# Eight of sixteen activation differences behind the last LSTM step: VectorE subtraction, or ScalarE negation and an adding DMA

## The chip, the cores and the metric

The kernel runs on one core of a Trainium2 chip. The time is the device time of one execution in microseconds (us). The kernel before was run three times: 306.83, 307.32 and 307.53 us, with a median of 307.32.

The core has five engines, each with an instruction queue of its own that runs in order: TensorE (PE: matrix products into the PSUM banks), VectorE (DVE), ScalarE (ACT), GpSimd (POOL) and SyncE (SP). Transfers (DMAs) are issued from the queues of SP, ACT and POOL and run by 16 DMA engines that all queues share. Semaphores hold an instruction back until what it needs is done; everything behind it in the same queue waits too.

## The reference

An LSTM over 64 time steps for 32 sequences with 256 hidden units, then a feed-forward net of three layers with weights of +1 and -1, and a residual:

```python
def step(carry, xw_t):
    prev_h, prev_c = carry
    a = xw_t + prev_h @ Wh
    i = sigmoid(a[:, :H]); f = sigmoid(a[:, H:2*H])
    o = sigmoid(a[:, 2*H:3*H]); g = tanh(a[:, 3*H:])
    next_c = f * prev_c + i * g
    next_h = o * tanh(next_c)
...
h = concatenate([y, -y], axis=-1)          # y: (32, 64, 256), the LSTM's output
h = relu(s0 * (h @ sign(k0))) * 2          # 512 -> 1024
h = relu(s1 * (h @ sign(k1))) * 2          # 1024 -> 1024
return x + s2 * (h @ sign(k2))             # 1024 -> 256
```

## The kernel before

**Blocks.** The 64 steps fall into four blocks of 16 steps; a block is 16 x 32 = 512 columns for the feed-forward net. The 64 recurrent steps run one after the other, and the products of the feed-forward net for blocks that are done are dealt out between them, as one long generator from which each step takes its share. The order of all instructions is written out by hand by that generator; each engine executes its own in that order.

**The last two blocks** are computed together by `last_blocks`. There, layer 1 (1024 to 1024) of both blocks is a product of a 2 x 2 matrix of weight quarters with a 2 x 2 matrix of activations, and is done with seven quarter products in place of eight (the Strassen-Winograd form). The activations are the layer-0 results: `f[k, 0]` for the third block and `f[k, 1]` for the fourth, k from 0 to 7, each a tile of 128 x 512 float32 (256 KB). With b11, b21 the lower and upper four tiles of the third block and b12, b22 those of the fourth, the form needs four differences, each of four tiles (K2 = 4), so sixteen in all:

- t1 = b12 - b11, written over `f[k, 0]`, k < 4 (L542)
- t2 = b22 - t1, in tiles of its own, `t2[k]` (L545)
- t3 = b22 - b12, written over `f[i, 1]`, i < 4 (L576)
- t4 = b21 - t2, written over `f[4 + i, 0]` (L586)

All four are made by `differ`, a VectorE subtraction (its records carry the line of the helper, L464).

**Splits.** Each operand of a product goes into TensorE as two float32r tiles, a high part and a low part. `split` (L481) makes them: a ScalarE cast into the high part (records at L482), and a VectorE subtraction, operand minus high, for the low part (again L464). The low part is issued one split later (`later`, L471), so that VectorE need not wait for the cast just before it.

**Order of the products behind the last step.** With four q banks, two banks that had held the gates, and two more (named r): t2's products into q0 to q3 (L573), then t1's into the same banks (L583), t3's into the four r banks (L594), t4's into the same (L601), b22's into q again (L607). Each product is eight matmuls (four parts, high and low) of 128 x 512. Between them:

- `u[i]` (L575) is a ScalarE copy of `q[i]` behind t2's product; t1's product then accumulates on in the same bank, so it must wait for the copy. `v[i]` (L585) is a copy of the same bank behind t1's product.
- `take_sum` (L496) adds `r[i]` to `v[i]` on VectorE (L497) behind t3's product; t4's product then accumulates on in r, and waits for that sum. The result goes through ReLU on ScalarE (L492) and a low part on VectorE (L493).
- layer 2 follows: the `po` products at L617 and L629, the output sums (L637) and the stores.

ScalarE's queue in this stretch, in order: the copies of `p1` into q2 and q3 (L560), four casts of t1, then for each i the copy `u[i]` and the cast of t3's part i, then for each i the copy `v[i]` and the cast of t4's part i, then casts of b22 mixed with the ReLUs of the sums.

GpSimd issues seven small loads at the start and computes some scales until about 12 us; its queue is empty from there to the end. SP issues the loads of the residuals (L96 by `load_x`, L565) just ahead of this stretch.

Of the kernel before, what the change touches and what calls it, by code (L numbers as in the profile page):

```python
# [37 lines left out]
AF = mybir.ActivationFunctionType  # L38
ALU = mybir.AluOpType
# [4 lines left out]
def lstm_ffn(ctx: ExitStack, tc: tile.TileContext, x, cond, wx_d, wh_d, b_d, k0_d, k1_d, k2_d, s0_d, s1_d, s2_d, out):  # L44
    nc = tc.nc
# [38 lines left out]
    def act(shape, dtype, name):  # L84
        return apool.tile(shape, dtype, tag="act", name=name)
# [312 lines left out]
    K2, F2 = FC0 // 2, F1 // 2  # L398
# [21 lines left out]

    f, parts = {}, {"b11": {}, "b21": {}}

    def layer0(p, m, hi, lo):
        for n, (k, a) in enumerate(((0, hi), (0, lo), (1, hi), (1, lo))):
            nc.tensor.matmul(p, w0[:, k, ts(m, P)], a[:, k, :], start=(n == 0), stop=(n == 3))  # L425
            if n < 3:
                yield 1

    def first_chunk(b, m):

        p = ps_f.tile([P, TB], F32, tag="pf", name=f"p0_{b}_{m}")
        yield from layer0(p, m, *hparts[b])
        f[m, 0] = act([P, TB], F32, f"f0_{m}")
        h, l = (act([P, TB], F32R, f"b{m}{s}") for s in "hl")
        load[0] += 1
        nc.scalar.activation(f[m, 0], p, AF.Relu)
        nc.scalar.copy(h, f[m, 0])
        nc.vector.tensor_tensor(l, f[m, 0], h, ALU.subtract)
        parts["b11" if m < K2 else "b21"][m % K2] = h, l
        yield 1  # L440

    def last_blocks(b):
# [6 lines left out]
        def product(bank, i, a, b, first=False):  # L449
            for k in range(K2):  # L450
                for n in range(2):
                    nc.tensor.matmul(  # L452
                        bank,
                        a(k)[:, ts(i, P)],
                        b[k][n],
                        start=first and k == 0 and n == 0,
                        stop=k == K2 - 1 and n == 1,
                        skip_group_check=True,
                    )
                    if not (k == K2 - 1 and n == 1):  # L460
                        yield 1

        def differ(out, in0, in1):
            nc.vector.tensor_tensor(out, in0, in1, ALU.subtract)  # L464

        def pair(name):
            return [act([P, TB], F32R, f"{name}{s}") for s in "hl"]
# [3 lines left out]
        def later(low):  # L471

            late.append(low)
            if len(late) > 1:
                late.popleft()()
# [5 lines left out]
        def split(a, h, l):  # L481
            nc.scalar.copy(h, a)  # L482
            later(lambda: differ(l, a, h))

        def large(name):

            both = [wpool.tile([P, K2, TB], F32R, tag=tag, name=f"{name}{tag}") for tag in ("wh", "w0")]
            parts[name] = [[t[:, k] for t in both] for k in range(K2)]
# [41 lines left out]
        t2 = [hpool.tile([P, 2, TB], F32, tag=tag, name=f"t2{tag}") for tag in ("hhi", "hlo")]  # L530
        t2 = [t2[k // 2][:, k % 2] for k in range(K2)]
        parts["t2"] = {}
        for n, m in enumerate(m for k in range(K2) for m in (k, K2 + k)):
            if n % 4 == 0:
                banks = four_banks(f"p0_{b + 1}_{n}_")
            p = banks[n % 4]
            yield from layer0(p, m, hi, lo)
            f[m, 1] = act([P, TB], F32, f"f1_{m}")
            nc.scalar.activation(f[m, 1], p, AF.Relu)
            k = m % K2  # L540
            if m < K2:
                differ(f[k, 0], f[k, 1], f[k, 0])  # L542
                yield 1
                continue
            differ(t2[k], f[m, 1], f[k, 0])  # L545
            for j in {0: [], K2 - 1: [k - 1, k]}.get(k, [k - 1]):
                parts["t2"][j] = pair(f"t2_{j}")
                split(t2[j], *parts["t2"][j])
            yield 1
            if k == 0:  # L550
                yield from second(1)
            else:
                settle()
            if k == 2:
                nc.scalar.copy(q[1], p1[1])
# [8 lines left out]
        for i in range(NQ):  # L564
            nc.sync.dma_start(out=res[i // 2][:, i % 2], in_=x_in[:, ts((b + 1) * NQ + i, SH)])  # L565

        large("t1")
        for k in range(K2):
            split(f[k, 0], *parts["t1"][k])
# [2 lines left out]
        for i in range(K2):  # L572
            yield from product(q[i], i, lambda k: sums[2, k], parts["t2"])  # L573
            u[i] = act([P, TB], F32, f"u{i}")
            nc.scalar.copy(u[i], q[i])  # L575
            differ(f[i, 1], f[K2 + i, 1], f[i, 1])  # L576
            parts["t3"][i] = pair(f"t3_{i}")
            split(f[i, 1], *parts["t3"][i])
            yield 1

        parts["t4"] = {}
        for i in range(K2):
            yield from product(q[i], i, lambda k: sums[1, k], parts["t1"])  # L583
            v[i] = act([P, TB], F32, f"v{i}")
            nc.scalar.copy(v[i], q[i])  # L585
            differ(f[K2 + i, 0], f[K2 + i, 0], t2[i])  # L586
            parts["t4"][i] = pair(f"t4_{i}")
            split(f[K2 + i, 0], *parts["t4"][i])
            yield 1
# [54 lines left out]
    def layer0_chunk(b, m):  # L644
        if b == NB - 2:
            yield from first_chunk(b, m)
            return
        p = ps_f.tile([P, TB], F32, tag="pf", name=f"p0_{b}_{m}")
        yield from layer0(p, m, *hparts[b])
        a0s[b, m] = evict(p, f"a0_{b}_{m}")  # L650
        yield 1
# [98 lines left out]
    def ffn():  # L750
        for b in range(NB - 2):
            yield from ffn_block(b)
        yield from last_blocks(NB - 2)
# [80 lines left out]
```

## Time and profile before

| | |
|---|---|
| median of three runs | 307.32 us |
| the profiled execution's own time | 307.09 us |
| its span on the core | 305.3 us |
| last recurrent step's matmuls (L308) end | about 232.5 us |
| t2's products into q | 249.27 to 256.52 us |
| t1's products into q | 256.52 to 263.77 us |
| t3's products into r | 263.77 to 271.03 us |
| t4's products into r | 271.03 to 278.28 us |
| b22's products into q | from 278.28 us |
| last matmul ends | 300.6 us |

The times are from the start of the span. The stages are read from the timeline of TensorE, as the start of the first matmul of each. The profile shows busy time for each engine; a matmul's record lasts 0.39 us, but the next starts 0.227 us after it, since they overlap. The chain that ended last is followed back from the last instruction: at each step to what released it, or to the instruction before it on its engine.

### The profile page before, as it was taken

What the parts mean: (1) busy time and instruction counts of PE and PEld (TensorE: products, weight loads), DVE (VectorE), ACT (ScalarE), POOL (GpSimd) and SP (SyncE); (2) the same over time, 40 slices, a digit from 0 to 9 for tenths busy, and PEclk for the clock granted to TensorE, in tenths of its full rate; (3) what the DMA queues carried; (4) which work ended last, traced back from release to release, by engine and by line L of the source; (5) the groups of instructions that cost most, each with busy time, mean ns of one, the idle gap of its engine ahead of it and who ended that gap; (6) DMA issues with size and microseconds to landing.
All of it is one profiled execution on the core that took longest, in us unless ns stands there. A gap on an engine that the chain in (4) does not pass through costs nothing.

```text
span 305.3 us, 9553 instructions
## 1 busy us (share of the span) xinstructions
PE 299.3 (98%) x4010; PEld 233.8 (77%) x4010; DVE 187.8 (62%) x527; ACT 154.9 (51%) x526; POOL 6.6 (2%) x24
## 2 busy tenths in 40 slices
PE   8999999999999999999999999999999999999993
PEld 4988887787777777777777777777777888888893
DVE  2476767676774565666575746444456689796341
ACT  0224657784565654444453544655676688644100
POOL 5300000000000000000000000000000000000000
PEclk9999999999999999999999999999999999999999
DMA  6865001133000000000001000000001330000012
GB/s 182 210 181 114 20 10 48 32 84 84 4 0 2 2 2 1 2 2 1 2 2 38 19 18 2 0 2 3 3 0 37 91 83 0 0 0 2 0 51 88
DMA packets 27450, 10.87 MB, mean 36 GB/s; under 512 B 23560, under 2 KB 26632, under 8 KB 27408
## 3 DMA queue, kind: packets, MB, share of 16 engines
q1 hardware_dynamic: 24768, 8.66, 11.5%
q10 hardware_dynamic: 2400, 1.57, 1.8%
q8 instruction: 31, 0.51, 0.7%
q0 software_dynamic: 240, 0.04, 0.1%
q14 instruction: 11, 0.09, 0.1%
HBM read 8.16 MB, written 2.10 MB: 34 GB/s over the span
## 4 chain that ended last, share of the span: by engine, by line
PE 98%; DVE 0%; issue 0%
PE p L679 21%; PE gates L308 20%; PE px L249 18%; PE q L452 12%; PE p L425 9%; PE po L666 5%; PE po L629 2%; PE gates L452 2%; PE po L617 2%; PE r L452 2%; PE gates L425 1%; PE p_idle L708 1%; PE gates L706 0%; DVE o L637 0%; PE p_bias L723 0%; DVE idle L113 0%
## 5 line engine op out<-in xcount | busy, mean ns | idle before, releaser
L308 PEld LDWEIGHTS gates<-wh,hist 128*32 128x32 f32 x2016 | 54.6, 109 | 22.3 <-issue 7.8
L308 PE MATMUL gates<-wh,hist 128*32 128x192 f32 x2016 | 68.1, 275 | 0.0
L249 PE MATMUL px<-wx,xT 128*32 128x256 f32 (+1 forms) x1168 | 60.5, 353 | 0.1
L249 PEld LDWEIGHTS px<-wx,xT 128*32 128x32 f32 x1168 | 42.4, 110 | 11.4 <-DVE c_first L717 0.8
L325 ACT ACTIVATE sig<-gates 128x128 f32<-128x128 f32 x64 | 17.7, 277 | 60.7 <-PE gates L308 60.4
L329 DVE TENSOR_TENSOR kept<-sig,c 128x64 f32<-128x64 f32 x63 | 14.2, 225 | 32.4 <-ACT sig L325 32.1
L335 ACT ACTIVATE th<-c 128x64 f32<-128x64 f32 x64 | 16.4, 257 | 32.2 <-DVE c L333 32.2
L337 DVE TENSOR_TENSOR h<-sig,th 128x64 f32<-128x64 f32 x64 | 14.4, 225 | 20.7 <-ACT th L335 20.7
L265 DVE TENSOR_TENSOR xg<-px,bias 128x512 f32<-128x512 f32 x32 | 21.2, 671 | 2.8 <-PE px L249 2.3
L425 PE MATMUL p<-hlo,w 128*128 128x512 f32 x56 | 22.5, 402 | 0.0
L425 PE MATMUL p<-hhi,w 128*128 128x512 f32 x56 | 22.3, 399 | 0.0
L319 ACT COPY gates<-xg 128x192 f32<-128x192 f32 x64 | 20.0, 313 | 0.6 <-DVE xg L265 0.6
L342 DVE STREAM_TRANSPOSE hist<-h 128x64 f32<-128x64 f32 x64 | 15.7, 246 | 2.6
L333 DVE TENSOR_TENSOR c<-kept,new 128x64 f32<-128x64 f32 x64 | 14.4, 225 | 2.2
L327 ACT ACTIVATE sig<-gates 128x64 f32<-128x64 f32 x64 | 14.9, 233 | 0.1
L331 DVE TENSOR_TENSOR new<-sig,cand 128x64 f32<-128x64 f32 x64 | 14.0, 218 | 0.0
L326 ACT ACTIVATE cand<-gates 128x64 f32<-128x64 f32 x64 | 14.0, 218 | 0.0
L320 ACT COPY gates<-xg 128x64 f32<-128x64 f32 x64 | 13.0, 203 | 0.0
L425 PEld LDWEIGHTS p<-hlo,w 128*128 128x128 f32 x56 | 10.5, 188 | 2.5
L425 PEld LDWEIGHTS p<-hhi,w 128*128 128x128 f32 x56 | 10.5, 188 | 2.4
L214 ACT ACTIVATE w<-bits,nsgn,sgn 128x1024 fp32r<-128x1024 uint8 x8 | 9.9, 1241 | 0.0
L362 DVE TENSOR_TENSOR hlo<-hist,hhi 128x256 fp32r<-128x256 f32 x16 | 7.5, 468 | 2.6 <-ACT hhi L361 2.6
(361 smaller groups left out, 573.4 us busy)
## 6 DMA issues: line engine op xcount, KB each, us to landing
x<-in_x_dram SPq DMA_DIRECT2D x52, 64.0 KB, 2.7
out_dram<-o SPq DMA_DIRECT2D x28, 64.0 KB, 1.8
bits<-in_L_ffn_k_dram SPq DMA_DIRECT2D x10, 128.0 KB, 3.4
wx<-in_L_cond_Wx_dram SPq DMA_DIRECT2D x2, 256.0 KB, 4.4
wx<-in_L_cond_Wx_dram ACTq DMA_DIRECT2D x4, 128.0 KB, 5.3
wh<-in_L_cond_Wh_dram ACTq DMA_DIRECT2D x2, 256.0 KB, 6.1
wh<-in_L_cond_Wh_dram SPq DMA_DIRECT2D x2, 256.0 KB, 6.8
k<-in_L_ffn_k_dram SPq DMA_DIRECT2D x2, 256.0 KB, 3.0
```

Of the source, the lines that this page charges most:

```text
L249: nc.tensor.matmul(p[q * N : (q + 1) * N, t % 2, slots], xT[i // 2, i % 2][:, s, k, :], wx_q[:, k, q, slots], start=start, stop=False, ski ...
L265: nc.vector.tensor_tensor(xg[t], p.rearrange("p t g j -> p t (g j)"), b, ALU.add)
L308: nc.tensor.matmul(g[q * N : (q + 1) * N], hT[:, k, :], wh_q[:, k, q, slots], start=False, stop=(k == 1), skip_group_check=True,)
L319: nc.scalar.copy(gates[0], x_t[:, :3])
L325: nc.scalar.activation(sig[:, 0:2, :], gates[0][:, 1:3], AF.Sigmoid)
L327: nc.scalar.activation(sig[:, 2, :], gates[1][:, 0], AF.Sigmoid)
L335: nc.scalar.activation(th, c, AF.Tanh)
L342: nc.vector.transpose(hT, h.rearrange("p (j b) -> p b j", b=2))
L425: nc.tensor.matmul(p, w0[:, k, ts(m, P)], a[:, k, :], start=(n == 0), stop=(n == 3))
L452: nc.tensor.matmul(bank, a(k)[:, ts(i, P)], b[k][n], start=first and k == 0 and n == 0, stop=k == K2 - 1 and n == 1, skip_group_check=True,)
L666: nc.tensor.matmul(po[m], w2[:, m, k], a1[k][n], start=(k == 0 and n == 0), stop=(k == FC1 - 1 and n == 1))
L679: nc.tensor.matmul(p1[m], w1[:, k, ts(m, P)], a0[k][n], start=(k == 0 and n == 0), stop=(k == FC0 - 1 and n == 1),)
```

## The change

The eight VectorE subtractions that make t3 and t4 are taken out. In place of each stands a ScalarE instruction that multiplies one operand by -1 in place, and a DMA, issued from GpSimd's queue, that reads one SBUF tile and adds it to another SBUF tile.

- t3: `f[i, 1]` is negated and `f[4 + i, 1]` is added to it. All four negations and DMAs are written ahead of the casts of t1.
- t4: `t2[i]` is negated and added to `f[4 + i, 0]`. These are written in the loop over t2's products, each behind the cast of t3's part i.

The four differences of t1 and the four of t2 stay on VectorE. The products and their order stay.

```diff
+    def negate(a):
+        nc.scalar.activation(a, a, AF.Copy, scale=-1.0)
+
+    def add_to(a, b):
+        nc.gpsimd.dma_start(out=a, in_=b, accum_op=ALU.add)
...
+        for i in range(K2):
+            negate(f[i, 1])
+            add_to(f[i, 1], f[K2 + i, 1])
         large("t1")
         for k in range(K2):
             split(f[k, 0], *parts["t1"][k])
...
             yield from product(q[i], i, lambda k: sums[2, k], parts["t2"])
             u[i] = act([P, TB], F32, f"u{i}")
             nc.scalar.copy(u[i], q[i])
-            differ(f[i, 1], f[K2 + i, 1], f[i, 1])
             parts["t3"][i] = pair(f"t3_{i}")
             split(f[i, 1], *parts["t3"][i])
+            negate(t2[i])
+            add_to(f[K2 + i, 0], t2[i])
             yield 1
...
             yield from product(q[i], i, lambda k: sums[1, k], parts["t1"])
             v[i] = act([P, TB], F32, f"v{i}")
             nc.scalar.copy(v[i], q[i])
-            differ(f[K2 + i, 0], f[K2 + i, 0], t2[i])
             parts["t4"][i] = pair(f"t4_{i}")
             split(f[K2 + i, 0], *parts["t4"][i])
             yield 1
```

In the program's order, ScalarE's queue becomes: the L560 copies, four negations, four casts of t1, then for each i: copy `u[i]`, cast of t3's part i, negation of `t2[i]`; then, as before, `v[i]` and the cast of t4's part i. Each cast of t3 and t4, and each low part of them on VectorE, waits for the DMA of its tile. GpSimd's queue gains eight DMAs behind its work at the start, each waiting for its negation.

## The prediction

> **What bounds the kernel now.** I read the page's busy shares and its chain that ended last, then, for the stretch behind the last step, the chain in order of time, then windows of five microseconds, then the timelines of ScalarE (ACT), VectorE (DVE) and GpSimd (POOL).
>
> ```profile
> PE 299.3 (98%) x4010; PEld 233.8 (77%) x4010; DVE 187.8 (62%) x527; ACT 154.9 (51%) x526; POOL 6.6 (2%) x24
> PE 98%; DVE 0%; issue 0%
> 245.80 18.13 PE q L452 x80
> 263.94 3.63 PE gates L452 x16
> ```
>
> TensorE (PE) is the bound: the chain is 98% its matmuls, and the last two lines, of the chain in order of time, show where the change sits: 80 matmuls in 18.13 us, 0.2267 us each, with no gap. They are the layer-1 products into q; the products into the banks called gates and r follow.
>
> ```profile
> 255.00:260.00 5.00, 5.00 (x24) 4.14 (x23) 5.00 (x10) 4.56 (x9) 0.00 (x0) 1.00 0.00 0
> 260.00:265.00 5.00, 5.00 (x24) 4.14 (x23) 3.62 (x6) 3.26 (x8) 0.00 (x0) 1.00 0.00 0
> 285.00:290.00 5.00, 5.00 (x24) 4.14 (x23) 1.39 (x3) 0.60 (x1) 0.00 (x0) 1.00 0.00 0
> ```
>
> Columns: stretch, length, then busy time of PE, weight load, DVE, ACT, POOL, granted clock, DMA share. DVE is full from 255 to 260, ACT nearly, and yet PE runs as many records (24) as from 285 to 290, where DVE does 1.39 us. So relieving DVE can't make PE faster: PE neither waits for it here nor slows beside it. DMA is empty throughout: new transfers meet no others.
>
> ```profile
> 250.15 1.26 ACT L560 COPY q<-p 128x512 f32<-128x512 f32 x2
> 251.35 2.18 ACT L482 CAST t1wh<-f 128x512 fp32r<-128x512 f32 x4
> 253.43 0.58 ACT L575 COPY u<-q 128x512 f32<-128x512 f32 x1
> 254.53 0.62 ACT L482 CAST t_0h<-f 128x512 fp32r<-128x512 f32 x1 [0.52 <-DVE f L464]
> 255.05 0.58 ACT L575 COPY u<-q 128x512 f32<-128x512 f32 x1
> ```
>
> This is the ACT queue into which the change goes. The cast of t3's part 0 follows the u0 copy, and u1 follows it. The u copies matter: each empties a q bank into which PE's t1 products accumulate again.
>
> **When PE wants its inputs** (start of the first matmul, PE timeline): q0 for t1 at 256.52, q1 at 258.33, q2 at 260.15, q3 at 261.96; t3's parts from 263.77 to 265.36; the bank of r0 for t4 at 271.03, then every 1.81 us.
>
> **The change, part by part.**
>
> Removed: eight DVE subtractions (L464, 0.69 us long, 0.605 from start to start), 4.8 us of DVE. By the windows above this buys nothing.
>
> Added, ACT: four negations ahead of the t1 casts and one behind each t3 cast. The nearest rows are the 128x512 casts and copies, 0.53 us from start to start; bounds 0.52 and 0.65 (spacing of the L482 and L560 pairs). The first four push t1's casts from 251.35 to 253.47 and u0 from 253.43 to about 255.6, ending 256.2; PE wants q0 at 256.52. Cost nothing with 0.3 us of cover, at most 0.2 by the 0.65. The t1 casts end near 255.7 and their DVE lows near 256.5, each ahead of its matmul (the last low is due at 258.11). The later four make ACT's loop (cast, negate, u copy) 1.6 us against PE's 1.81: no cost either, unless the cast waits.
>
> Added, POOL's queue: eight DMAs of 256 KB, SBUF to SBUF with an add. Nothing else stands in that queue behind 12 us. Nothing waits behind them but the end of the program. SP's loads and stores are unmoved.
>
> Added, waits: ACT's cast of each t3 or t4 part now waits for its DMA, not a DVE subtraction. Behind the t3 cast in the ACT queue stand the next negation (which releases a t4 DMA) and the next u copy (for which PE waits). Behind the t4 casts stand the v copies, the b22 casts and the ReLUs of c. On DVE the lows of t4 wait too, and behind them stand the sums v += r (L497), which PE waits for before it accumulates t4 into r.
>
> **Price of a DMA.** The trace has no adding DMA and none within SBUF, so two unknowns: L, from issue to landing of the first, and B, the time from one landing to the next when they queue.
>
> ```profile
> h_first<-in_cond_dram POOLq DMA_DIRECT2D x1, 32.0 KB, 4.6
> s<-in_L_ffn_s_dram POOLq DMA_DIRECT2D x3, 0.5 KB, 5.4
> res<-in_x_dram SPq DMA_DIRECT2D x4, 128.0 KB, 2.8
> wh<-in_L_cond_Wh_dram SPq DMA_DIRECT2D x2, 256.0 KB, 6.8
> 6.00:7.00 1.00, 1.00 (x45) 1.00 (x40) 0.00 (x0) 0.00 (x0) 0.00 (x0) 1.00 0.93 297
> 5.00:6.00 1.00, 1.00 (x18) 0.43 (x20) 0.34 (x2) 0.00 (x0) 0.28 (x1) 1.00 1.00 263
> ```
>
> L: low 2.8 (res), high 6.8 (wh, same size, behind other loads). I take 5.0, between the 4.6 and 5.4 of POOL's own queue: these moved little but met full rings; ours carries 256 KB through empty ones. B: the last figure of the two window lines is GB/s, so 256 KB moved once needs 0.88 us at 297 or 1.0 at 263. Low 0.88. An add must also read its destination: twice the 1.0 is 2.0, which I take. Three passes (two reads and a write, none overlapped) give 3.0; with no overlap of one DMA with the next, B is L's low end, 2.8, or more; I keep 4.0 as the far end, since nothing in the trace excludes it.
>
> [...]
>
> **The sum.** The first negation ends at 251.95, so POOL issues at 252.0 and DMA j lands at 252.0 + L + jB where they queue. (DMA 4 is released by the negation behind t3's first cast, 1.2 us after DMA 0 lands; with B = 2.0 the queue is still three deep, so they do queue.) DMA 7 lands at 252.0 + 5.0 + 14.0 = 271.0. Then the ACT cast 0.62 and its handover 0.04, the DVE low 0.605 to the next DVE start, v0 += r0 0.69, handover 0.05: 2.0 in all, so PE may start t4 into r0 at 273.0 in place of 271.03: 2.0 late. The following sums come every 2.05 us (265.79, 267.79, 269.84, 271.89 in the DVE timeline) against PE's 1.81, and where they used to have slack, three of them now add 0.23 each: 0.7. Added: 2.7 us. In general it is L + 7B − 16.3, and from the u copies alone L − 4.6 (cast 0.53, negation 0.53, copy 0.58 and handovers behind DMA 0's landing, against 258.33). The larger counts; at L 5.0 and B 2.0 the second asks 0.4, inside the 2.7. Behind this PE runs gap-free again to 300.57, and all behind it shifts whole.
>
> The profiled execution took 307.09 (span 305.3): 309.8. The runs' median is 307.32, 0.23 above it, so I say 310.0.
>
> **Rivals.**
> - Transfers land in time (the other side): with B under 1.6 and L under 4.6 both formulas are negative; POOL's queue has been idle for 240 us and the rings are empty, which speaks for it; that all four of POOL's kinds of row need 4.6 or more speaks against. Time 307.3, as before.
> - Only the first is late: B under 1.6 but L 5.0 to 6.2. PE waits for u1: 0.4 to 1.6 us, 307.7 to 308.9. For it: POOL's 5.4 row. Against: it needs an add at nearly the price of a plain move.
> - The adds are slow: B 3.0 to 4.0, so 5.0 + 21.0 − 16.3 = 9.7, and 16.7 at 4.0: 317 to 324. For it: nothing in the trace shows an add. PE would also wait for u2, u3 and t3. Against: only lack of overlap gives it.
> - Faster: the DVE time freed would have to reach PE. The windows show 24 records per 5 us whether DVE is full or idle, so there is nothing to gain: 307.3 less noise.
>
> **Chances.** Forecast (B 1.7 to 2.6 at L 5.0, so 0.6 to 6.9 us; its own range 307.9 to 314.2) 0.43; adds slow (or between) 0.21; first late 0.15; in time 0.17; faster 0.04. What can be told from no change is about 0.2%, 0.6 us: of the third case 0.02 falls within it. So slower 0.77, same 0.19, faster 0.04. The range reaches down to 306.9, to take in no change, and up to 317.0, the slow adds at B 3.0 (9.7 on 307.3); outside are the slower adds (0.09) and faster (0.04).
>
> **What would show it.** Right: PE idle between 256 and 279, put down to v L497's sums and u copies, with the ACT casts of t3 and t4 idle for DMAs; landing rows for POOL's DMAs that grow from 5 us to about 9 as they queue; a DMA share well up from 252 to 271; everything up to 251.35 and after the last wait alike. Wrong: PE's chain unbroken, so L under 4.6 and B under 1.6; waits first at u1 only; a B beyond 3, with stalls at u2, u3 and t3 too; or DVE or PE rows that lengthen while the transfers run, which the sum holds at nothing. A wait of PE for u0 at 256.5 would show negations longer than 0.6 us.

## The result and the profile after

The changed kernel takes 307.71 us (median of 18 runs, 307.06 to 308.82) where the kernel before, run beside it, takes 307.13 (18 runs, 306.83 to 307.75). The ratio is 1.0018, with a 95% interval from 1.0009 to 1.0026: some 0.55 us slower, a fifth of the 2.7 us that the prediction added. 307.71 lies in its range, near the lower end. The profiled execution took 307.82 us with a span of 305.8, against 307.09 and 305.3 before.

The page first: the busy shares, the chain that ended last by engine, and the queue of GpSimd's DMAs.

```profile
PE 298.4 (98%) x4010; PEld 233.7 (76%) x4010; DVE 183.3 (60%) x519; ACT 158.5 (52%) x534; POOL 13.6 (4%) x32
PE 96%; DMA 1%; SPq 0%; DVE 0%; issue 0%
q0 software_dynamic: 1392, 2.14, 3.9%
```

DVE lost eight records, ACT and POOL gained eight each. The chain is still TensorE's, but 1% of it is now a DMA; where that DMA stands is the surprise further down. It is not one of the eight.

The chain in order of time (start, length, what), behind the last step:

```profile
246.30 18.13 PE q L458 x80
264.44 3.63 PE gates L458 x16
301.10 0.48 DVE o L646
```

Here the prediction failed. The 80 matmuls into q took 18.13 us before and take 18.13 now; the 16 of t3 and t4 that follow, now at L458, took 3.63 and take 3.63. There is no gap for a copy u and none for a sum. From the first recurrent product (L308) to the start of the last matmul it is 283.60 us before and 283.62 after.

The windows behind it (stretch, length, busy time of PE, weight load, DVE, ACT, POOL with counts, then granted clock, DMA share and GB/s):

```profile
255.00:260.00 5.00, 5.00 (x24) 4.14 (x23) 3.47 (x6) 5.00 (x11) 2.83 (x4) 1.00 1.07 193
260.00:265.00 5.00, 5.00 (x24) 4.14 (x23) 2.77 (x4) 4.88 (x11) 2.03 (x3) 1.00 0.98 177
265.00:270.00 5.00, 5.00 (x24) 4.14 (x23) 3.54 (x6) 3.21 (x6) 0.00 (x0) 1.00 0.12 21
```

PE runs its 24 records per 5 us at a granted clock of 1.00, as before, though the share of the DMA engines went from 0.00 to about 1. DVE fell from 5.00 to 3.47 us in the first window: the relief is real and buys nothing. By about 266 the transfers are over.

The DMAs in the timeline of POOL (start, length, what, idle time before it and what ended that), and the DMA issues on the page, whose last figure is the median time from issue to landing:

```profile
252.78 3.65 POOL L427 DMA_DIRECT2D f<-f  x4 [241.09 <-ACT f L424]
257.94 0.85 POOL L427 DMA_DIRECT2D f<-t2hhi  x1 [1.50 <-DVE t_0l L470]
259.46 0.86 POOL L427 DMA_DIRECT2D f<-t2hhi  x1 [0.67 <-DVE t_1l L470]
260.99 0.85 POOL L427 DMA_DIRECT2D f<-t2hlo  x1 [0.67 <-DVE t_2l L470]
262.51 0.86 POOL L427 DMA_DIRECT2D f<-t2hlo  x1 [0.67 <-ACT t2hlo L424]
...
f<-f POOLq DMA_DIRECT2D x4, 256.0 KB, 4.5
f<-t2hhi POOLq DMA_DIRECT2D x2, 256.0 KB, 3.8
```

The first four landed 3.3, 4.2, 4.9 and 5.8 us after their issues, at 256.1, 257.6, 258.9 and 260.3: 1.4 us apart, while POOL began to issue them 0.5 to 0.6 apart. Those are the numbers that the prediction lacked. Counted from its release (the first negation ends at 252.47), the first DMA takes 3.6 us: L is 3.6, not 5.0, and B is 1.4, not 2.0. t4's four were issued 1.52 us apart, wider than 1.4, so no queue built up among them; each took 3.8. (Three of their brackets name a VectorE low as what ended POOL's wait. The negation of the same part ended 0.3 us before each issue too, as before the first of t3, so the trace doesn't tell which of the two released them.) The last landed at 266.3, 13.8 us behind the first release; the prediction had 19.0.

ScalarE's timeline:

```profile
251.85 2.19 ACT L424 ACTIVATE f<-f 128x512 f32<-128x512 f32 x4
253.94 2.17 ACT L488 CAST t1wh<-f 128x512 fp32r<-128x512 f32 x4
256.02 0.57 ACT L584 COPY u<-q 128x512 f32<-128x512 f32 x1
256.50 0.62 ACT L488 CAST t_0h<-f 128x512 fp32r<-128x512 f32 x1
...
266.34 0.62 ACT L488 CAST t_3h<-f 128x512 fp32r<-128x512 f32 x1 [0.41 <-DMA f<-t2hlo]
```

The first matmuls that need q0 for t1 and r0 for t4, in PE's timeline, and between them the sum v0 += r0, in DVE's:

```profile
257.02 0.39 PE L458 MATMUL q<-t1wh,s 128*128 128x512 f32 x1
...
267.61 0.68 DVE L503 TENSOR_TENSOR v<-gates,v 128x512 f32<-128x512 f32 x1
...
271.53 0.39 PE L458 MATMUL gates<-t_0h,w 128*128 128x512 f32 x1
```

The four negations take 2.19 us together. The copy u0 ends at 256.59; PE wants its bank at 257.02 (256.52 in the profile before, and this stage starts 0.5 later). The cast of t3's part 0 at 256.50 follows the copy at once, with no wait in brackets: its DMA landed 0.4 us earlier. The only wait for one of the eight DMAs in the profile is the last line's 0.41 us, for the last of t4, and it reaches nobody: the sum v0 += r0 ends at 268.29, and PE wants r0 for t4 at 271.53. The landings left 3.2 us of slack there.

**Where the half microsecond is.** The two profiles agree in length from the recurrence on, so their 0.49 us of difference in span lies ahead of it. The start of the chain in order of time, first of before, then of after:

```profile
2.27 3.37 PE p_idle L708 x8
5.64 1.89 PE px L249 x64
```

```profile
1.65 4.55 DMA wx<-in_L_cond_Wx_dram
6.20 0.14 issue
6.34 3.70 PE px L249 x128
```

After the change the first products waited for a load of wx, 250 us ahead of the first changed instruction. A single profile can't say whether that is the change or chance, so the experiments measure it over many runs.

### The profile page after: what moved, and what is told of

The parts are those of the page before. It is cut to its first block, busy times and chain, and to the rows that moved or that the text cites. A ratio compares the mean times of both kernels' runs of the same rounds, so it can differ in the third digit from the quotient of the medians.

```text
span 305.8 us, 9577 instructions
## 1 busy us (share of the span) xinstructions
PE 298.4 (98%) x4010; PEld 233.7 (76%) x4010; DVE 183.3 (60%) x519; ACT 158.5 (52%) x534; POOL 13.6 (4%) x32
## 3 DMA queue, kind: packets, MB, share of 16 engines
q0 software_dynamic: 1392, 2.14, 3.9%
## 4 chain that ended last, share of the span: by engine, by line
PE 96%; DMA 1%; SPq 0%; DVE 0%; issue 0%
PE p L688 21%; PE gates L308 20%; PE px L249 18%; PE q L458 12%; PE p L431 9%; PE po L675 5%; PE po L638 2%; PE po L626 2%; PE r L458 2%; PE gates L458 2%; DMA wx<-in_L_cond_Wx_dram 1%; PE gates L431 1%; SPq L96 0%; DVE o L646 0%; PE p_bias L732 0%
## 5 line engine op out<-in xcount | busy, mean ns | idle before, releaser
L308 PEld LDWEIGHTS gates<-wh,hist 128*32 128x32 f32 x2016 | 54.6, 109 | 22.3 <-issue 7.8
L308 PE MATMUL gates<-wh,hist 128*32 128x192 f32 x2016 | 68.1, 275 | 0.0
L427 POOL DMA_DIRECT2D f<-f x4 | 3.7, 1436 | 241.1 <-ACT f L424 241.1
```

The lines of the kernel that those rows point to most:

```text
L308: nc.tensor.matmul(g[q * N : (q + 1) * N], hT[:, k, :], wh_q[:, k, q, slots], start=False, stop=(k == 1), skip_group_check=True,)
```

## The experiments

All runs, each beside runs of the kernel before on the same chip. "Outside" is a run's time less its span, as a mean; the last column has the records of the trace in the queues of POOL and ACT, 39 and 684 in the kernel before.

| run | median us | ratio [95%] | span, mean | outside | POOL, ACT |
|---|---|---|---|---|---|
| before, again (e1) | 307.12 | 0.9998 [0.9983, 1.0013] | 305.45 | 1.77 | 39, 684 |
| after, again (e2) | 307.88 | 1.0017 [1.0001, 1.0032] | 305.80 | 2.01 | 59, 693 |
| adds on DVE, no DMA (e3) | 307.19 | 0.9997 [0.9988, 1.0006] | 305.39 | 1.79 | 39, 688 |
| before + spare DMAs (e4) | 309.98 | 1.0085 [1.0069, 1.0101] | 308.04 | 1.77 | 53, 684 |
| the same, spare tile last (e5) | 307.27 | 1.0007 [0.9992, 1.0022] | 305.63 | 1.79 | 53, 684 |
| before less 8 subtractions (e6) | 307.32 | 1.0005 [0.9994, 1.0016] | 305.63 | 1.80 | 39, 680 |
| t3 negated late (e7) | 308.79 | 1.0045 [1.0031, 1.0059] | 306.9 | 2.01 | 59, 692 |
| t4 in place (e8) | 321.56 | 1.0479 [1.0453, 1.0506] | 319.98 | 2.00 | 59, 690 |
| t3's DMAs alone (e9) | 307.31 | 1.0007 [0.9996, 1.0018] | 305.62 | 1.79 | 51, 689 |
| DMAs copy (e10) | 307.59 | 1.0014 [0.9999, 1.0029] | 305.73 | 2.01 | 59, 693 |
| 480 columns (e11) | 307.90 | 1.0020 [1.0006, 1.0034] | 305.78 | 2.13 | 59, 695 |
| negations alone (e12) | 307.29 | 0.9999 [0.9990, 1.0007] | 305.48 | 1.79 | 39, 690 |
| before + 20 on POOL (e13) | 307.35 | 1.0004 [0.9994, 1.0014] | 305.39 | 2.04 | 59, 684 |
| before + 60 on POOL (e14) | 307.28 | 1.0001 [0.9992, 1.0010] | 305.45 | 1.78 | 99, 684 |
| before + 11 on ACT (e15) | 307.60 | 1.0007 [0.9998, 1.0016] | 305.35 | 2.12 | 39, 695 |
| after + 40 on POOL (e16) | 307.53 | 1.0009 [0.9995, 1.0022] | 305.71 | 1.80 | 99, 693 |

**Do the DMAs or the negations cost anything?** e1 and e2 are the two kernels unchanged. e3 keeps order, negations and queues but makes the sums on DVE; e12 leaves the sums out.

> The kernel before, unchanged, as a null run. Every theory: ratio 1.000 within its interval, near 307.1 us. It gives a second profile of the start: in the first pair of profiles the whole difference of 0.5 us lies ahead of 20 us (TensorE's first 128x128 products with wx at 5.58 before, at 6.34 after). If the start alone varies by half a microsecond between executions of one kernel, this profile may show its first product anywhere from 5.5 to 6.5.

> The changed kernel, unchanged. Theory S (the 0.18% of the first comparison are real, made by the DMAs on GpSimd's queue or the four microseconds of ACT work, outside the stage of the change): ratio 1.0010 to 1.0026 again, and again more time than before ahead of the change. Theory N (a draw of the start's jitter): ratio 0.9995 to 1.0008. Both: no gap of TensorE from 249 to 290 us.

```diff
-        nc.gpsimd.dma_start(out=a, in_=b, accum_op=ALU.add)
+        nc.vector.tensor_tensor(a, a, b, ALU.add)      # e3
+        pass                                           # e12
```

> Negations stay on ACT, the add is made by VectorE in the place of the DMA; no DMA on GpSimd's queue is added. Theory S with the DMAs as cause: ratio 1.000. Theory S with ACT's negations as cause: ratio 1.0018. Theory N: 1.000. TensorE without a gap in the stage in all.

> The changed kernel with the negations and without the DMAs, so with no addition: the instruction counts of the changed kernel on ACT and VectorE, none more on GpSimd. If the counts of ACT and VectorE together make the 0.23 us outside the span and the 0.3 us inside: 2.01, 305.7, ratio 1.0018. If the DMAs make them: 1.78, 305.4, ratio 1.000.

Both e3 and e12 lie at the time before (0.9997 and 0.9999). So eight more instructions on ACT, ahead of t1's casts and inside the u loop, cost nothing measurable, and whatever the change costs comes with the eight DMAs, through their work or through the records that they add to POOL's queue.

**Is there anything to gain from DVE?** e6 leaves the eight subtractions of t3 and t4 out and puts nothing in their place.

```diff
-            differ(f[i, 1], f[K2 + i, 1], f[i, 1])
...
-            differ(f[K2 + i, 0], f[K2 + i, 0], t2[i])
```

> The kernel before without the eight subtractions of t3 and t4, which are left out of the computation: VectorE has the instruction count of the changed kernel, and there is no negation and no DMA. Theory I: span 305.7 to 305.9, time minus span 2.01. Theory D: span 305.4, time minus span 1.78, ratio 1.000. Both: relieving VectorE of 4.8 us gains nothing, ratio not below 0.9990.

The ratio is 1.0005 with 1 well inside its interval: not even removing the work altogether makes the kernel faster.

**What would a late landing have cost?** Two kernels take the slack away. e7 puts t3's negations and DMAs behind the casts of t1; e8 leaves t3 alone and puts t4's negation and DMA directly ahead of the cast that needs them.

```diff
-        for i in range(K2):
-            negate(f[i, 1])
-            add_to(f[i, 1], f[K2 + i, 1])
         large("t1")
         for k in range(K2):
             split(f[k, 0], *parts["t1"][k])
+        for i in range(K2):
+            negate(f[i, 1])
+            add_to(f[i, 1], f[K2 + i, 1])
```

> The changed kernel with t3's four negations and DMAs written behind the casts of t1 in place of ahead of them, so 2.1 us later. Theory M (landing 3.3 us behind the issue, the rest as the prediction had it): DMA 0 lands at 257.7 in the clock of the kernel before, the cast of t3 waits, u1 ends at 259.4 where TensorE wants the bank at 258.33: one stall of 1.0 to 1.1 us at q1, nothing more, so 308.7 us, ratio 1.005 against before. Rival (the ACT queue or t4's chain has slack that takes it up): 307.8, ratio 1.002. Rival (a stall also at the sums v += r): 2 us and more.

The waits of e7 between 250 and 300 us (engine, tile and line, releaser: total us, times, longest):

```profile
ACT t_0h L488 <- DMA f<-f: 1.6, 1, 1.6
...
PEld q L458 <- ACT u L584: 1.3, 1, 1.3
...
PE q L458 <- ACT u L584: 0.9, 1, 0.9
```

The wait of ACT for the DMA reaches PE through the copy u1, the first of the two ways that the prediction names. In PE's timeline the matmuls lose 1.06 us there and 0.11 more in one slower matmul, 1.17 in all; the mean span grew by 1.1 us over e2's. The rule "L − 4.6" is thus confirmed with a different L: with the measured 3.6 and a release 2.1 us later it gives 3.6 + 2.1 − 4.6 = 1.1.

```diff
-            negate(t2[i])
-            add_to(f[K2 + i, 0], t2[i])
             yield 1
...
             nc.scalar.copy(v[i], q[i])
+            negate(t2[i])
+            add_to(f[K2 + i, 0], t2[i])
             parts["t4"][i] = pair(f"t4_{i}")
```

> The changed kernel with t4's negation and DMA where the subtraction had stood, right ahead of the cast that needs it. Theory M: ACT waits out each DMA (negation 0.6, handover 0.3, landing 3.3, cast and copy 1.1, so 5.3 us a part), the last of four lands near 281, and TensorE starts t4 into r0 near 283 in place of 271: 12 to 13 us, 319 to 321 us, ratio 1.039 to 1.044. Rival (DMAs overlap since the next negation does not depend on the cast): under 6 us.

The waits of e8 in the same stretch, and then five of its windows:

```profile
PE gates L458 <- DVE v L503: 11.4, 1, 11.4
...
ACT t_3h L488 <- DMA f<-t2hlo: 3.6, 1, 3.6
...
ACT t_0h L488 <- DMA f<-t2hhi: 3.5, 1, 3.5
```

```profile
271.00:275.00 4.00, 0.77 (x4) 0.31 (x2) 0.69 (x1) 1.31 (x3) 0.86 (x1) 0.88 0.28 52
275.00:279.00 4.00, 0.00 (x0) 0.00 (x0) 0.69 (x1) 1.63 (x3) 0.86 (x1) 0.50 0.08 14
285.00:287.00 2.00, 2.00 (x6) 1.61 (x5) 1.84 (x4) 1.14 (x2) 0.00 (x0) 0.50 0.00 0
287.00:289.00 2.00, 2.00 (x8) 1.58 (x8) 1.90 (x4) 1.14 (x2) 0.00 (x0) 0.82 0.00 0
289.00:291.00 2.00, 2.00 (x10) 1.66 (x9) 1.90 (x4) 0.64 (x1) 0.00 (x0) 1.00 0.00 0
```

With the queue gone, ACT waits some 3.5 us for every DMA, and four such waits in a row hold PE, through the sums into v (L503), for 11.4 us: the second way that the prediction names. The idle time is what was expected, with t4 into r0 from 283.2 us on; the time lies above the expected 319 to 321 us through the clock, which the expectation left out. While PE idles the granted clock falls to 0.50, and when PE starts again it does 6 records in 2 us in place of 10, until the clock is back at 1.00. Two estimates from the windows say when: the mean of 0.88 over the first puts the fall near 274.0, some 2.3 us after the last matmul's end at 271.8, and that of 0.82 from 287 to 289 puts the return near 287.7, some 4.5 us after PE's start. Half the clock for 4.5 us is some 2.3 us lost, an estimate too; with the 11.4 us of idle time that makes nearly all of the 13.8 by which e8 is above the changed kernel. The prediction's prices for the slow rivals, with some 10 to 17 us of stalls, left the clock out.

**What does an add cost beside a copy?** e10 leaves the add out of the DMA, so that t3 and t4 are plain copies; e9 keeps t3's four DMAs alone; e11 transfers 480 of 512 columns.

```diff
-        nc.gpsimd.dma_start(out=a, in_=b, accum_op=ALU.add)
+        nc.gpsimd.dma_start(out=a, in_=b)                                           # e10
+        nc.gpsimd.dma_start(out=a[:, :480], in_=b[:, :480], accum_op=ALU.add)       # e11
```

> The changed kernel with the eight DMAs as plain copies, the addition left out of the computation. It prices the add itself. If the add doubles a DMA's traffic, as the prediction took it: four in a row land 0.7 us apart in place of 1.4, the first after 2.6 to 2.9 us in place of 3.3. If it costs nothing: 1.4 apart, 3.3 the first. The time stays 307.5 to 307.9 in both, as nothing waits for them; outside the span 2.01 if the add is not what makes it, 1.78 if it is.

> The changed kernel with t3 alone by negation and DMA; t4's four subtractions are back on VectorE. The three kernels with all eight DMAs into the activations had 0.23 us more outside the span (2.01 against 1.78 to 1.80) and, stalls taken off, spans near 305.7 against 305.4. If that goes with the number of DMAs or of instructions: 1.89 outside, span 305.55. If it is a step that the first such DMA makes: 2.01 and 305.7. If it needs t4's DMAs: 1.78 and 305.4. TensorE's chain is unbroken in the stage in each case.

> The changed kernel with DMAs of 480 of the 512 columns (240 KB, rows of 1920 bytes, as in e5); 32 columns are not added. If the rows' length makes the 0.23 us outside the span: 1.78. If not: 2.01. Landings 0.1 us shorter. Time 307.1 to 307.9.

e10, from the page and POOL's timeline:

```profile
q0 software_dynamic: 880, 2.14, 1.8%
...
f<-f POOLq DMA_DIRECT2D x4, 256.0 KB, 2.6
f<-t2hhi POOLq DMA_DIRECT2D x2, 256.0 KB, 2.2
```

```profile
252.53 2.27 POOL L427 DMA_DIRECT2D f<-f  x4 [240.75 <-ACT f L424]
257.70 0.54 POOL L427 DMA_DIRECT2D f<-t2hhi  x1 [2.90 <-DVE t_0l L470]
```

The same bytes, 2.14 MB, take 1.8% of the 16 DMA engines as copies and 3.9% as adds. Before the change that queue took 0.1%, so a copy takes 1.7% of 305.5 us over eight, 0.65 us, and an add 3.8% of 305.8 over eight, 1.45 us: 2.2 times as much. POOL's record of an issue is 0.54 us against 0.85. The first copy lands in 2.3 us, the first add in 3.3; t3's four copies land some 0.8 us apart, the adds 1.4. So the doubling in the prediction was right, and the pass that it doubled was not: 0.65 us, where it read 1.0 from windows in which other loads shared the rings.

And yet e10, with half the transfer, gains nothing sure on e2 (1.0014 against 1.0017, intervals wide), and e9, with half the DMAs, is at the time before. Nothing here shows that what remains of the 0.55 us goes by bytes. With 240 KB, e11's DMAs of t4 land in 3.6 to 3.7 us in place of 3.8, and its time stays where the changed kernel's is.

**A trap: eight spare DMAs.** e4 runs eight adding DMAs, one after the other, into a spare tile in the kernel before. e5 is the same with the tile in a pool allocated last.

```diff
+    spare = const.tile([P, 480], F32, name="spare")
+    nc.gpsimd.memset(spare, 0.0)
...
+        for i in range(2 * K2):
+            nc.gpsimd.dma_start(out=spare, in_=f[K2 + i % K2, 1][:, :480], accum_op=ALU.add)
         large("t1")
```

> The kernel before, with eight adding DMAs of 240 KB onto a spare tile that nothing reads, one after the other, at the same place; all subtractions stay on VectorE. Theory S with the DMAs as cause: ratio 1.0015 to 1.0026, with TensorE's chain unbroken in the stage. Theory N or ACT as cause: ratio 1.000. The DMA rows also price one adding DMA alone: 3.3 to 3.8 us from issue to landing.

> The eight adding DMAs of 240 KB of e4 beside the kernel before, but with the spare tile allocated last, so that no other tile moves (in e4 it pushed the tiles behind it by 1920 bytes, and TensorE's matmuls ran slower from 84 us on, long before the DMAs). Theory D (DMAs on GpSimd's queue cost the changed kernel its 0.4 us in the span and 0.23 us outside it, wherever they write): span median 305.7 to 305.9, time minus span 2.01, ratio 1.0015 to 1.0025. Theory I (it is the number of instructions on an engine): span 305.4, time minus span 1.78, ratio 1.000. Theory A (the tile's address slowed e4): no slope against the kernel before; if the DMAs slowed TensorE, the slope of e4 comes back.

e4 took 2.6 us more, which looked as if the transfers slowed TensorE after all. Its chain in order of time shows otherwise:

```profile
273.08 3.73 PE gates L454 x16
...
287.78 7.44 PE po L621 x32
```

The 32 `po` products in the kernel before, and in e5:

```profile
285.70 7.25 PE po L617 x32
...
286.10 7.25 PE po L622 x32
```

3.73 in place of 3.63 and 7.44 in place of 7.25, with no wait; and both stretches lie behind the last DMA, issued at 269.2: the last five issues stand 3.4 us apart, each but the first of them released by the landing of the one ahead. Most of the loss lies ahead of the first of those DMAs (issued at 242.2): the `p_bias` products start at 9.66 us in place of 9.55, and a run of 17 matmuls into q at 234.12 in place of 232.53. The matmuls stand further apart: the 512-column ones of the `po` products 232.5 ns from start to start in place of 226.6 (7.44 and 7.25 us over 32), those into gates and r 229.7 in place of 226.6 (14.70 and 14.50 us over 64). The spare tile had moved every tile allocated behind it by 1920 bytes. In e5, with the same DMAs and the other tiles back in place, the `po` spacing is 226.6 again and the ratio 1.0007. So adding DMAs and GpSimd's issues beside TensorE cost nothing measurable, and e4's loss came with the addresses of the tiles that moved; by the trace it is 2.2 us in the profiled execution.

**The 0.23 us outside the span.** In the table, "outside" is 1.77 to 1.80 in the kernel before and in most variants, and 2.00 to 2.01 in after, e2, e7, e8, e10, whether the DMAs add or copy. All of these have 59 records in POOL's queue; e5, with eight DMAs and 53 records, has 1.79. e13, e14 and e15 add tiny instructions to the kernel before, on a tile that nothing reads, e16 to the kernel after:

```diff
+    spare = spool.tile([P, 64], F32, name="spare")
+    for i in range(20):      # e13; 60 in e14, 40 in e16
+        nc.gpsimd.memset(spare[:, i : i + 1], 0.0)
...
+        for i in range(11):  # e15 instead, ahead of the last products
+            nc.scalar.copy(spare[:, i : i + 1], total)
```

> The kernel before with twenty more tiny GpSimd memsets behind its work at the start, on a spare tile allocated last; no DMA, no negation. Theory P (the length of GpSimd's instruction stream, 59 records, makes the time outside the span, whatever the instructions are): time minus span 2.01; if the 0.25 us inside come from it too, span 305.7. Theory Q (it needs the DMAs): 1.79 and 305.4.

> Sixty more GpSimd memsets, 99 records. Theory P with a cost in steps by the block: 2.01 or one or more steps of 0.12 to 0.23 above it. Theory P with a single threshold: 2.01. Theory Q: 1.79.

> The kernel before with eleven more tiny ScalarE copies just ahead of the last products, where ScalarE is idle: 695 records on ACT. Theory P for ACT (e11's 0.12 come from ACT's stream passing 693 records): time minus span 1.90 to 1.92. Rival: 1.79.

> The changed kernel with forty tiny GpSimd memsets more at the start, 99 records in its queue as in e14. If the count alone makes the time outside the span: time minus span 1.78 in place of 2.01, and ratio 1.0005 to 1.0012 in place of 1.0018. If the DMAs have a part in it: 2.01 stays. The 0.25 us inside the span: span mean 305.7 to 305.8 if they go with the DMAs, 305.5 if they were a draw of the start or went with the count.

e13 has no DMA of the change and 59 records, and its time outside the span is 2.04: the whole 0.23, without the DMAs. With 99 records it is back at 1.78 (e14), and the changed kernel padded to 99 has 1.80 (e16). e15 shows the same on ACT: 695 records, 2.12, as in e11, which has 695 there too and 59 on POOL, and still 2.13, not the sum of both. So this part of the loss goes with the number of records in a queue, in no simple order, and not with the DMAs' work. Why, these runs don't tell.

**The rest, inside the span, is open.** The five kernels with the change's eight DMAs and no stall (after, e2, e10, e11, e16) have a mean span of 305.75 us (63 runs, standard error 0.07); the kernel before has 305.51 (142 runs, 0.035), and the other variants at its level 305.49 (90 runs, 0.04): 0.24 more, with a standard error of 0.08. From the first recurrent product to the last matmul their profiles are alike, 283.55 to 283.63 us, as in the kernel before (only e1, the kernel before again, has 283.99). So, as far as one profile of each can tell, the 0.24 us lie at the start, in the loads that the first products wait for. There the first product came at 6.25 us or later in four of the seven kernels with the change's eight DMAs (after, e7, e8, e11), and at 5.5 to 6.0 in the other three and in all eleven others. That fits, but it is one draw of each. Other runs don't settle it: against the runs of the kernel before beside it, e5, with eight DMAs of its own, has 0.20 us more span (standard error 0.22), and e6, with none, has 0.20 more too (0.15). No run singled out the cause.

## Why the prediction was right or wrong

- *PE is the bound and DVE's relief buys nothing:* right. 24 records per 5 us at either DVE load, and e6 at 1.0005.
- *Negations at no cost:* right. Predicted spacing 0.53 us, measured 0.52 to 0.53; u0 was to end 0.3 us ahead of PE's need and ended 0.43 ahead; e12 at 0.9999.
- *POOL's queue, and the order of the waits:* right in kind. Only casts wait for DMAs, and e7 and e8 show that the wait would go to PE by just the two ways named, u1 and the sums into v.
- *Price of a DMA:* **this step failed, in both its terms.** L was taken at 5.0, between the 4.6 and 5.4 of POOL's own rows, though the text itself said that those rows met full rings; in the empty rings of this stage the adding DMA landed 3.6 us behind its release (3.3 behind its issue). The low row, 2.8, was nearer. That other transfers lengthen a landing shows in t4's adds: 3.2 us where each ran alone (e8), 3.8 where the one ahead was still under way (the changed kernel). B was taken at 2.0, twice 1.0; the doubling held (2.2 times), but the single pass is 0.65 us of the engines (copies land 0.8 apart), and the adds landed 1.4 apart.
- *The sum:* the formula stood; its inputs didn't. L + 7B − 16.3 gives 5.0 + 14.0 − 16.3 = 2.7 as predicted and 3.6 + 9.8 − 16.3 = −2.9 as measured. L − 4.6 gives −1.0. The first is near the 3.2 us of slack seen at r0. Either error alone would have left a stall (L 3.6 with B 2.0: 1.3 us by the first formula; L 5.0 with B 1.4: 0.4 by the second), so it took both to lose it. That the DMAs queue from the first to the last also failed, since at 1.4 they keep pace with t4's releases 1.52 apart.
- *Rivals:* "transfers land in time" is what happened in the stage, by its own condition, B under 1.6 and L under 4.6, and by the sign that the prediction named as showing its forecast wrong, PE's chain unbroken. It had less than half the chance of the forecast. Its time, 307.3, is 0.4 under the 307.71.
- *The sign:* the ratio puts the change 0.55 us above, just under the 0.6 that the prediction counted as told from no change, and not for the reason given. It falls into 0.23 outside the span, which e13 and e16 show to be no work of the DMAs, and some 0.24 inside it, likely at the start, open; the rest is within the spread of the runs. Neither was in any of the cases.

## What to carry to other kernels

Price a transfer by rows whose rings are as full as those it will meet: landings of about 5 us at a crowded start were no price for an empty stage, where the adding DMA landed in 3.3 us. Crowding is shown to lengthen a landing, from 3.2 us to 3.8 between e8's adds of t4 and the changed kernel's; the rows at the start also read from DRAM, and what that adds no run shows. Before betting on a stall, write the landing against the need of the queue behind it and ask how far off each of the two inputs must be; here 30% in both was enough. When a change moves a kernel by 0.2%, split the time into the span and what lies around it, and pad the unchanged kernel to the same number of instructions, before giving the loss to the work that was added.

## What the runs showed of the hardware

- The time outside the span goes with the number of records in an engine's queue, without order: POOL 39, 51 and 53: 1.8 us; 59: 2.0; 99: 1.8; ACT 695: 2.1.
- Moving the tiles behind a spare one by 1920 bytes slowed 512-column matmuls by up to 6 ns of 227 (e4's `po` products), 2.6 us in all by the ratio of the runs, with no wait shown; with those tiles back in place the `po` spacing was 226.6 again (e5). Which tile matters wasn't tried.
- An adding DMA within SBUF takes 2.2 times the DMA engines' time of a copy of the same bytes (1.45 against 0.65 us for 256 KB) and 0.85 against 0.54 us of POOL's issue; four in a row land 1.4 us apart, copies 0.8. An add of 256 KB lands in 3.2 us alone (e8) and in 3.8 where the one ahead is still under way (the changed kernel).
- In 11.4 us of idle TensorE the granted clock fell to 0.50, some 2.3 us after the last matmul, and some 4.5 us of work went by before it was 1.00 again (e8; both times are estimates from the mean clock of a window, 0.88 from 271 to 275 us and 0.82 from 287 to 289).
